# A four-layer graph network on one core: slot waits by tile, layer 3 scaled and added in one VectorE pass, transposes back and stores one tick later

## The chip, the cores and the metric

The kernel runs on one core of a Trainium2 chip. The metric is device time in microseconds (us), the median over several executions. Five engines work from queues of their own, in order: TensorE (PE in the profile, PEld its weight loads), VectorE (DVE), ScalarE (ACT), GpSimd (POOL) and SyncE (SP, which here only issues DMAs). An instruction that waits holds up everything behind it on its engine.

## The reference, cut to what matters

`x` is (16, 1024, 256), `adj` a sparse 1024 x 1024 matrix used by all layers, everything in float32.

```
layer 0: S = sigmoid(relu(x_u W1a + x_v W1b + b1) . W2 + b2)   for every pair u, v
         a = (S * adj)^T x ;  m = (adj^T x) * x
         z = beta1 x + beta2 (a Wa + ba) + beta3 (m Wm + bm)
layer 1: z = z + relu((adj z) W^T + b)
layer 2, 3: f = z W1^T ; s = f . W2 + b2
         c = softmax(leaky_relu(s_i + s_j) + adj) over j
         z = c f + bias2 + z
```

## The kernel before, in words

The first part loads `adj` into `adj_sb`, picks up to 32 edges of every row with VectorE (`slot_a`), and projects four batches on TensorE (`first_group`, `edge_sides`: for each tile of 128 nodes four matmuls, each of which shows as two records, then two ScalarE copies into `st`, and for every second tile three stores `u_d`, `v_d`, `hw_d` on SP's queue). A generator, `work`, deals these tiles out: `more(n)` issues the next n of them. After the row search it has four tiles left. Then come the counts that decide whether the edge lists fit: `full` (L461), two small matmuls (L464, L466), `missed`, a third (L484), and `ok`. Every engine reads `ok` and branches.

The second part (from L683) opens pools of its own on the bytes that the first part's pools gave up. It begins by transposing `adj` (L225, copied into `stage` by L138 and L140), and then works through batches in four groups of four. Beside TensorE's dense work a generator, `Side`, deals out the edge scores of layer 0 at hand-set paces (`PACE`): a gather by GpSimd (L703), two VectorE passes over 128 x 1024 (L820, L822), four ScalarE sums (L826), later a scatter (L708). `paced` ties a step of it to a recent matmul.

A group does layer 0's sums with edges (`with_edges`), layer 1, and then layers 2 and 3 as `front` (projection, L128 with tile `g_wT`) and `sums` (L1089 builds a weight tile `m` on VectorE, L128 with `feats` and `m` sums over eight `jt`). A `sums` covers 512 nodes, so a batch has two, v = 0 and v = 1. At its end `finish` takes four accumulators `acc`, each in a bank of its own of PSUM's eight; column D of an accumulator holds the softmax's denominator.

- Layer 2 (`second`): four reciprocals (L1104), four scaled copies `val` on ScalarE (L1266), and `turn_back`: eight transposes (L1273) and two VectorE adds into `z` (L1277).
- Layer 3 (`third`): the same four reciprocals, scaled copies `st` (L1312), one VectorE add per pair of tiles with the residual that was transposed into PSUM by `early` (L1300, L1316), and a store from ScalarE's queue (L1317).

`later` is a list of steps with countdowns; `tick` counts all of them down and runs those at its head that are due:

```
def tick():
    for what in later:
        what[0] -= 1
    while later and later[0][0] <= 0:
        later.pop(0)[1]()
```

A `front` ticks at jt = 1 and 5, a `sums` at jt = 0, 2, 4 and 6. Besides `turn_back` the list holds `to_row` (due at the next tick) and `from_row` (due at the fifth), which turn a projection's scores into a row.

Of the kernel before, what the change touches and what calls it, by code (L numbers as in the profile page):

```python
# [1 line left out]

# [7 lines left out]
F32 = mybir.dt.float32  # L10
I32 = mybir.dt.int32
U32 = mybir.dt.uint32
AF = mybir.ActivationFunctionType
ALU = mybir.AluOpType
AX = mybir.AxisListType
P = 128
# [15 lines left out]
LEAD = 4  # L32
# [35 lines left out]
def gnn_stack_kernel(  # L68
# [41 lines left out]
    def bank():  # L110
        return psum[-1].tile([P, HN], F32, tag="bank", name="bank")
# [260 lines left out]
    with ExitStack() as stack:  # L372
# [61 lines left out]
        def more(n):  # L434
            for _ in range(n):
                next(work, None)
# [23 lines left out]
        for q in range(NG):  # L460
            nc.vector.tensor_scalar(full[:, q, :], slot_a[:, :, FIRST + QUAD * q], 0.0, None, ALU.is_gt)  # L461
        flags = full.rearrange("p g t -> p (g t)")
        ps = bank()
        nc.tensor.matmul(ps[:, :NF], below, flags, start=True, stop=True)  # L464
        ps2 = bank()
# [14 lines left out]
        nc.vector.tensor_tensor(missed, counts[:, 0:1], counts[:, 1:2], ALU.not_equal)  # L480
        nc.vector.tensor_tensor(missed, missed, counts[:, 3:4], ALU.add)
        nc.vector.scalar_tensor_tensor(missed, counts[:, 2:3], TOP, missed, ALU.is_gt, ALU.add)
        ps3 = bank()
        nc.tensor.matmul(ps3[:, :1], ones, missed, start=True, stop=True)  # L484
        total = prep1.tile([P, NF], F32, name="total")
# [197 lines left out]
    with tc.If(listed > 0) as arm:  # L683
        with ExitStack() as stack:
# [3 lines left out]

            zs = stack.enter_context(tc.tile_pool(name="zs", bufs=2))
            slot_pool = stack.enter_context(tc.tile_pool(name="slots", bufs=LEAD + 2))
            wide_z = stack.enter_context(tc.tile_pool(name="wide_z", bufs=4))
            wide_t = stack.enter_context(tc.tile_pool(name="wide_t", bufs=5))
            psum_pool(stack, "banks", 8)
            gd_pool = stack.enter_context(tc.tile_pool(name="gd", bufs=4))
            gc_pool = stack.enter_context(tc.tile_pool(name="gc", bufs=2))
            put = [Scatters(tc, f"scores {g}") for g in range(NGR)]
            finished = []
            TW = NT * (D + 1)  # L700
# [221 lines left out]
            doing = ["free"]  # L922

            with ExitStack() as first:
                own1 = first.enter_context(tc.tile_pool(name="own1", bufs=1))
                st_pool = first.enter_context(tc.tile_pool(name="st", bufs=2))
                side = Side(score_steps(own1))
                pools = (wide_t, wide_z)
                next_up = load_kept(pools, 0)
                wm = load_wm(own1, nc.sync)  # L930
                zero = own1.tile([P, ZERO], F32, name="zero")
                nc.gpsimd.memset(zero, 0.0)

                def stage(n):
                    return st_pool.tile([P, 2 * 3 * D], F32, tag="st", name="stage")[:, :n]

                def score_free():
                    yield from turn_adj(
                        lambda n: wide_z.tile([P, DH * N], F32, tag="wide", name="stage")
                    )  # L940
                    h, hT = next_up
                    for b in range(B):
                        if b == 1:
                            nat = load_naturals(stage)
                            w1 = load_w1(own1, nc.sync)
                        if b == 2:
                            paced(with_beta2(w1))
                        if b >= GB:
                            yield from edge_sides(st_pool, b, w1, hT)
                        if b == B - 1:  # L950
                            first_hw.extend(load_hw(i) for i in range(GB - 1))
                            first_gd.extend(load_gd(0, 0, ut) for ut in range(4))
                        mT = yield from messages(pools, h, hT)
                        now = hT

                        if b + 1 < GB:
                            h, hT = load_kept(pools, b + 1)
                        elif b + 1 < B:
                            h = load_h(pools[0], b + 1)
                            hT = turned(pools[0], h)  # L960
                            yield 2.4
                        yield from without_edges(pools, b, now, mT, wm)
                        if b == 1:
                            prepare(nat)
                            yield 3

                def with_zeros(main):
                    for n, us in enumerate(main):
                        if 7 < n < 40 or n > 40 and n % 3 == 0:
                            clear()  # L970
                        yield us

                side.along(with_zeros(score_free()))
                assert not zeros

            two = stack.enter_context(tc.tile_pool(name="two", bufs=2))
            three = stack.enter_context(tc.tile_pool(name="three", bufs=3))
            four = stack.enter_context(tc.tile_pool(name="four", bufs=4))


            ea = adj_sb
# [6 lines left out]
            def tick():  # L988
                for what in later:
                    what[0] -= 1  # L990
                while later and later[0][0] <= 0:
                    later.pop(0)[1]()

            def catch_up():
                while later:
                    later.pop(0)[1]()
# [82 lines left out]
            def sums(made, v, finish, early=None):  # L1079

                doing[0] = "sums"
                while "f" not in made:
                    tick()
                f, r, ta = made["f"], made["r"], made["ta"]
                cols = slice(v * HN, (v + 1) * HN)
                acc = [bank() for _ in range(HT)]
                for jt in range(NT):
                    m = four.tile([P, HN], F32, tag="m", name="m")
                    nc.vector.scalar_tensor_tensor(  # L1089
                        m, r[:, cols], ta[:, jt : jt + 1], ea[:, jt, cols], ALU.max, ALU.mult  # L1090
                    )
                    for c in range(HT):
                        product(
                            acc[c][:, : D + 1], m[:, c * P : (c + 1) * P], f[:, jt, :],
                            start=jt == 0, stop=jt == NT - 1,
                        )
                    if jt % 2 == 0:
                        tick()
                    if early:
                        early(v, jt)  # L1100
                    yield 1.7
                share = small.tile([P, HT], F32, tag="share", name="share")
                for c in range(HT):
                    nc.vector.reciprocal(share[:, c : c + 1], acc[c][:, D : D + 1])  # L1104
                finish(v, acc, share)
                yield 1.2

            def exponential(jt):
# [147 lines left out]


            def second(z, i):
                def finish(v, acc, share):
                    cols = slice(v * HN, (v + 1) * HN)  # L1260
                    vals = []
                    for c in range(HT):
                        if c % 2 == 0:
                            pair = four.tile([P, 2, D], F32, tag="st", name="val")
                        val = pair[:, c % 2, :]
                        nc.scalar.activation(val, acc[c][:, :D], AF.Identity, scale=share[:, c : c + 1])  # L1266
                        vals.append(val)

                    def turn_back():
# [6 lines left out]
                        for dh in range(DH):  # L1276
# [1 line left out]
                                z[i][:, dh, cols], ps[dh], gat2.bias2[:, dh : dh + 1], z[i][:, dh, cols],  # L1278
                                ALU.add, ALU.add,
                            )  # L1280
                    later.append([1, turn_back])
                return finish


            def third(z, i, b):
# [17 lines left out]
                            )  # L1303
                    turned_back.append(ps)

                def finish(v, acc, share):
                    for c in range(0, HT, 2):
                        ps = turned_back.pop(0)
                        it = v * HT + c
                        st = four.tile([P, 2, D], F32, tag="st", name="st")  # L1310
                        for k in range(2):
                            nc.scalar.activation(  # L1312
                                st[:, k, :], acc[c + k][:, :D], AF.Identity, scale=share[:, c + k : c + k + 1]
                            )
                        both = st.rearrange("p t d -> p (t d)")
                        nc.vector.tensor_tensor(both, both, ps, ALU.add)  # L1316
                        nc.scalar.dma_start(  # L1317
                            out[b + i, it * P : (it + 2) * P].rearrange("(t p) d -> p t d", p=P), st
                        )
                return finish, early  # L1320

            def pair_layers(b, z, first):
# [13 lines left out]
                yield from sums(m0, 1, *t0)  # L1336
                yield from sums(m1, 0, *t1)
                yield from sums(m1, 1, *t1)
                assert not later

            def group_layers(g, z):

# [25 lines left out]
                        soon(g + 1)  # L1368
                    yield from sums(made[layer, i], 1, *ends)
                loaded.append((hw, nz))  # L1370
                assert not later

            def soon(g):

# [165 lines left out]
```

## Time and profile before

| | us |
|---|---|
| median of 3 runs | 3192.23 (3180.22 to 3192.65) |
| the profiled execution: time, span | 3160.66, 3159.0 |
| TensorE matmul busy | 3089.6 (98%) |
| VectorE busy | 2355.8 (75%) |
| ScalarE busy | 1954.7 (62%) |
| GpSimd busy | 1853.1 (59%) |

The profiled execution was 20 to 32 us shorter than the three timed ones. Busy shares are averages over stages: the first part ends near 110 us, the four groups begin near 953, 1517, 2074 and 2636 us, and the edge scores run beside all but the last.

### The profile page before, as it was taken

How to read it: one execution, taken by the hardware profiler on the slowest of the kernel's cores; microseconds unless marked ns; L12 is line 12 of the kernel's file. 1: busy time of each engine (PE TensorE's matmuls, PEld its weight loads, DVE VectorE, ACT ScalarE, POOL GpSimd, SP SyncE). 2: the span in 40 equal slices, each digit the busy share in tenths (PEclk: the TensorE clock that was granted, in tenths of full speed). 3: DMA queues.
4: the chain of work that ended last, by engine and by line, in shares of the span. 5: the costliest groups of instructions: out<-in, count | busy, mean ns of one | idle time of the engine just before them, and what ended most of it. 6: DMA issues, size and time to landing. Idle time of an engine off the chain costs nothing. (4 is left out here: it accounts for less than half of the span.)

```text
span 3159.0 us, 38968 instructions
## 1 busy us (share of the span) xinstructions
PE 3089.6 (98%) x11954; PEld 2178.2 (69%) x11954; DVE 2355.8 (75%) x3191; ACT 1954.7 (62%) x6512; POOL 1853.1 (59%) x1483
## 2 busy tenths in 40 slices
PE   9899999999999999999999999999999999999999
PEld 5444555545547756888875688888557888858888
DVE  7796777768774678999767899976789982148844
ACT  3245565656667876777987677788667764514242
POOL 1146877667664577767666776756766651076600
PEclk9999999999999999999999999999999999999999
DMA  9799798788889777568877765787765655485500
GB/s 323 286 331 324 251 308 283 256 258 251 259 278 327 229 216 206 150 186 261 294 233 203 207 167 166 262 277 232 223 197 149 162 189 174 130 254 166 165 5 28
DMA packets 288420, 699.96 MB, mean 222 GB/s; under 512 B 46141, under 2 KB 141178, under 8 KB 281034
## 3 DMA queue, kind: packets, MB, share of 16 engines
q0 software_dynamic: 128224, 387.80, 42.1%
q1 hardware_dynamic: 132538, 258.46, 23.5%
q10 hardware_dynamic: 27440, 51.13, 4.3%
q8 instruction: 96, 1.57, 0.2%
q14 instruction: 122, 1.00, 0.1%
HBM read 565.83 MB, written 131.41 MB: 221 GB/s over the span
## 5 line engine op out<-in xcount | busy, mean ns | idle before, releaser
L826 ACT ACTIVATE z<-z 128x256 f32<-128x256 f32 x2432 | 978.9, 405 | 573.3 <-DVE z L822 544.9
L820 DVE TENSOR_TENSOR z<-z,u 128x1024 f32<-128x1024 f32 x608 | 739.0, 1220 | 392.9 <-PE bank L128 284.6
L128 PE MATMUL bank<-feats,m 128*128 128x257 f32 x4096 | 915.5, 381 | 12.8 <-DVE m L1089 7.1
L703 POOL DMA_INDIRECT z<-v_d,slot_v x512 | 652.1, 1274 | 434.8 <-ACT z L826 249.7
L128 PEld LDWEIGHTS bank<-feats,m 128*128 128x128 f32 x4096 | 767.9, 190 | 128.7 <-DVE m L1089 13.4
L708 POOL DMA_INDIRECT dense_d<-gt,slot_at x512 | 665.8, 1300 | 192.7 <-issue 128.9
L822 DVE SCALAR_TENSOR_TENSOR z<-z,w2r 128x1024 f32<-128x1024 f32 x608 | 737.9, 1220 | 9.0
L128 PE MATMUL bank<-gc,hw 128*128 128x256 f32 x2048 | 451.7, 382 | 9.5 <-ACT gc L1120 8.2
L826 ACT ACTIVATION_READ_ACCUMULATOR z<-z 128x1 f32 x2432 | 460.0, 189 | 0.0
L128 PE MATMUL bank<-adj_sb,h 128*128 128x512 f32 x1024 | 444.0, 594 | 2.6 <-ACT st L330 2.6
L128 PEld LDWEIGHTS bank<-gc,hw 128*128 128x128 f32 x2048 | 386.6, 190 | 73.9 <-ACT gc L1120 19.7
L1089 DVE SCALAR_TENSOR_TENSOR m<-rho,tau,adj_sb 128x512 f32<-128x512 f32 x512 | 376.1, 744 | 68.1 <-PE bank L128 65.3
L128 PE MATMUL bank<-adjT_in,y 128*128 128x512 f32 (+1 forms) x960 | 403.3, 580 | 4.6 <-DMA adjT_in<-adjT_d 4.6
L128 PEld LDWEIGHTS bank<-adj_sb,h 128*128 128x128 f32 x1024 | 194.9, 191 | 243.0 <-issue 238.7
L128 PE MATMUL bank<-w,hT 128*128 128x512 f32 (+1 forms) x1024 | 336.8, 490 | 0.0
L128 PEld LDWEIGHTS bank<-adjT_in,y 128*128 128x128 f32 x960 | 182.2, 191 | 219.3 <-issue 200.6
L1120 ACT ACTIVATE gc<-gd 128x1024 f32<-128x1024 f32 x128 | 264.8, 2070 | 88.7 <-PE bank L128 72.7
L128 PEld LDWEIGHTS bank<-w,hT 128*128 128x128 f32 x1024 | 196.1, 192 | 142.5 <-issue 118.8
L128 PE MATMUL bank<-g_wT,z 128*128 128x257 f32 x1024 | 233.7, 380 | 3.4 <-ACT st L1312 2.3
L128 PEld LDWEIGHTS bank<-g_wT,z 128*128 128x128 f32 x1024 | 191.0, 190 | 34.9 <-ACT st L1312 4.3
L703 POOL DMA_INDIRECT z<-v_d,x_node x96 | 119.9, 1249 | 131.6 <-ACT z L826 89.8
L330 ACT ACTIVATE st<-bank 128x512 f32<-128x512 f32 x128 | 75.7, 591 | 103.0 <-PE bank L128 63.4
(168 smaller groups left out, 2369.5 us busy)
## 6 DMA issues: line engine op xcount, KB each, us to landing
gd<-dense_d SPq DMA_DIRECT2D x128, 512.0 KB
dense_d<-zero ACTq DMA_DIRECT2D x64, 512.0 KB
adjT_in<-adjT_d SPq DMA_DIRECT2D x112, 256.0 KB
h<-in_x_dram SPq DMA_DIRECT2D x19, 1024.0 KB
u_d<-st SPq DMA_DIRECT2D x64, 256.0 KB
v_d<-st SPq DMA_DIRECT2D x64, 256.0 KB
hw_d<-st SPq DMA_DIRECT2D x64, 256.0 KB
u<-u_d POOLq DMA_DIRECT2D x32, 512.0 KB
```

The source lines that it names most:

```text
L128: recent.append(nc.tensor.matmul(*args, **kw))
L330: nc.scalar.activation(st[:, c, :2, :], ps.rearrange("p (s k) -> p s k", s=2), AF.Copy)
L703: return nc.gpsimd.indirect_dma_start(out=dst, out_offset=None, in_=src[:], in_offset=bass.IndirectOffsetOnAxis(ap=at, axis=0), **how,)
L708: return nc.gpsimd.indirect_dma_start(out=dst[:], out_offset=bass.IndirectOffsetOnAxis(ap=at, axis=0), in_=src, in_offset=None,)
L820: paced(nc.vector.tensor_tensor(z, z, u, ALU.add))
L822: nc.vector.scalar_tensor_tensor(zk, zk, 0.0, w2r[:, None, :].to_broadcast([P, GB, D]), ALU.max, ALU.mult)
L826: nc.scalar.activation(zk[:, c, :], zk[:, c, :], AF.Copy, accum_out=s[:, k, c : c + 1])
L1089: nc.vector.scalar_tensor_tensor(m, r[:, cols], ta[:, jt : jt + 1], ea[:, jt, cols], ALU.max, ALU.mult)
L1120: paced(nc.scalar.activation(gc, gd.rearrange("p n i -> p i n"), AF.Copy), 16)
```

## The change

Every SBUF pool of the second part (`zs`, `slots`, `wide_z`, `wide_t`, `gd`, `gc`, `own1`, `st`, `two`, `three`, `four`) is opened with `reuse_waits="tile"`. Without it, a pool that lands on bytes of released pools waits, with all its tiles, for every user of those pools. With it, a tile waits for the users of earlier tiles on its own bytes alone. The pool in PSUM stays as it was.

In the first part two tiles of `work` are issued before the first count matmul and one before the third; one is left for the end.

`tick` runs whatever is due, wherever it stands in the list. `turn_back` gets 2 for its countdown instead of 1; layer 2's `finish` makes its four reciprocals itself, as `sums` did, and its `val` tiles grow by the unused column. Layer 3 copies each accumulator with its denominator (257 columns) unscaled on ScalarE, takes the reciprocals of a pair from that copy, and scales and adds the residual in one VectorE pass per tile. Its store goes into `later` with a countdown of 1. What is left in the list at a group's end is run there.

```diff
+        more(2)
         ps = bank()
         nc.tensor.matmul(ps[:, :NF], below, flags, start=True, stop=True)
...
+        more(1)
         ps3 = bank()
         nc.tensor.matmul(ps3[:, :1], ones, missed, start=True, stop=True)
...
-            zs = stack.enter_context(tc.tile_pool(name="zs", bufs=2))
+            zs = stack.enter_context(tc.tile_pool(name="zs", bufs=2, reuse_waits="tile"))
...
-                while later and later[0][0] <= 0:
-                    later.pop(0)[1]()
+                for what in [w for w in later if w[0] <= 0]:
+                    later.remove(what)
+                    what[1]()
...
-                share = small.tile([P, HT], F32, tag="share", name="share")
-                for c in range(HT):
-                    nc.vector.reciprocal(share[:, c : c + 1], acc[c][:, D : D + 1])
-                finish(v, acc, share)
+                finish(v, acc)
...
-                    later.append([1, turn_back])
+                    later.append([2, turn_back])
...
-                        st = four.tile([P, 2, D], F32, tag="st", name="st")
+                        st = four.tile([P, 2, D + 1], F32, tag="st", name="st")
+                        share = small.tile([P, 2], F32, tag="share", name="share")
                         for k in range(2):
-                            nc.scalar.activation(
-                                st[:, k, :], acc[c + k][:, :D], AF.Identity, scale=share[:, c + k : c + k + 1]
-                            )
-                        both = st.rearrange("p t d -> p (t d)")
-                        nc.vector.tensor_tensor(both, both, ps, ALU.add)
-                        nc.scalar.dma_start(
-                            out[b + i, it * P : (it + 2) * P].rearrange("(t p) d -> p t d", p=P), st
-                        )
+                            nc.scalar.activation(st[:, k, :], acc[c + k][:, : D + 1], AF.Copy)
+                        nc.vector.reciprocal(share, st[:, :, D])
+                        for k in range(2):
+                            nc.vector.scalar_tensor_tensor(
+                                st[:, k, :D], st[:, k, :D], share[:, k : k + 1], ps[:, k * D : (k + 1) * D],
+                                ALU.mult, ALU.add,
+                            )
+                        to = out[b + i, it * P : (it + 2) * P].rearrange("(t p) d -> p t d", p=P)
+                        later.append([1, functools.partial(nc.scalar.dma_start, to, st[:, :, :D])])
...
-                assert not later
+                catch_up()
```

More of the change, by code (lines that the diff above doesn't have):

```diff
@@ L1 @@
+import functools
 from contextlib import ExitStack
@@ L684, in gnn_stack_kernel @@
         with ExitStack() as stack:
-            zs = stack.enter_context(tc.tile_pool(name="zs", bufs=2))
-            slot_pool = stack.enter_context(tc.tile_pool(name="slots", bufs=LEAD + 2))
-            wide_z = stack.enter_context(tc.tile_pool(name="wide_z", bufs=4))
-            wide_t = stack.enter_context(tc.tile_pool(name="wide_t", bufs=5))
+            zs = stack.enter_context(tc.tile_pool(name="zs", bufs=2, reuse_waits="tile"))
+            slot_pool = stack.enter_context(tc.tile_pool(name="slots", bufs=LEAD + 2, reuse_waits="tile"))
+            wide_z = stack.enter_context(tc.tile_pool(name="wide_z", bufs=4, reuse_waits="tile"))
+            wide_t = stack.enter_context(tc.tile_pool(name="wide_t", bufs=5, reuse_waits="tile"))
             psum_pool(stack, "banks", 8)
-            gd_pool = stack.enter_context(tc.tile_pool(name="gd", bufs=4))
-            gc_pool = stack.enter_context(tc.tile_pool(name="gc", bufs=2))
+            gd_pool = stack.enter_context(tc.tile_pool(name="gd", bufs=4, reuse_waits="tile"))
+            gc_pool = stack.enter_context(tc.tile_pool(name="gc", bufs=2, reuse_waits="tile"))
             put = [Scatters(tc, f"scores {g}") for g in range(NGR)]
@@ L924, in gnn_stack_kernel @@
             with ExitStack() as first:
-                own1 = first.enter_context(tc.tile_pool(name="own1", bufs=1))
-                st_pool = first.enter_context(tc.tile_pool(name="st", bufs=2))
+                own1 = first.enter_context(tc.tile_pool(name="own1", bufs=1, reuse_waits="tile"))
+                st_pool = first.enter_context(tc.tile_pool(name="st", bufs=2, reuse_waits="tile"))
                 side = Side(score_steps(own1))
@@ L974, in gnn_stack_kernel @@
                 assert not zeros
-            two = stack.enter_context(tc.tile_pool(name="two", bufs=2))
-            three = stack.enter_context(tc.tile_pool(name="three", bufs=3))
-            four = stack.enter_context(tc.tile_pool(name="four", bufs=4))
+            two = stack.enter_context(tc.tile_pool(name="two", bufs=2, reuse_waits="tile"))
+            three = stack.enter_context(tc.tile_pool(name="three", bufs=3, reuse_waits="tile"))
+            four = stack.enter_context(tc.tile_pool(name="four", bufs=4, reuse_waits="tile"))
             ea = adj_sb
@@ L1258, in second, with finish @@
             def second(z, i):
-                def finish(v, acc, share):
+                def finish(v, acc):
                     cols = slice(v * HN, (v + 1) * HN)
+                    share = small.tile([P, HT], F32, tag="share", name="share")
+                    for c in range(HT):
+                        nc.vector.reciprocal(share[:, c : c + 1], acc[c][:, D : D + 1])
                     vals = []
@@ L1263, in finish @@
                         if c % 2 == 0:
-                            pair = four.tile([P, 2, D], F32, tag="st", name="val")
-                        val = pair[:, c % 2, :]
+                            pair = four.tile([P, 2, D + 1], F32, tag="st", name="val")
+                        val = pair[:, c % 2, :D]
                         nc.scalar.activation(val, acc[c][:, :D], AF.Identity, scale=share[:, c : c + 1])
@@ L1304, in early, with finish @@
                     turned_back.append(ps)
-                def finish(v, acc, share):
+                def finish(v, acc):
                     for c in range(0, HT, 2):
@@ L1370, in group_layers @@
                 loaded.append((hw, nz))
-                assert not later
+                catch_up()
             def soon(g):
```

## The prediction

> **What bounds the kernel now.** I read the busy shares first, then TensorE's waits, then the timeline around the largest of them.
>
> ```profile
> span 3159.0 us, 38968 instructions
> PE 3089.6 (98%) x11954; PEld 2178.2 (69%) x11954; DVE 2355.8 (75%) x3191; ACT 1954.7 (62%) x6512; POOL 1853.1 (59%) x1483
> ```
>
> TensorE is busy for 98%, so the change can only give what TensorE idles or runs slowly: 3159.0 - 3089.6 = 69 us, of which some 7.5 are the first loads and 7 the tail. Who holds it, from the waits of engine PE (total, times, longest):
>
> ```profile
> PE bank L128 <- ACT st L1312: 8.4, 13, 1.5
> PE bank L1273 <- ACT val L1266: 7.4, 6, 2.2
> PE bank L128 <- DVE m L1089: 7.1, 8, 2.3
> PE bank L464 <- DVE full L461: 4.0, 1, 4.0
> PE bank L225 <- ACT stage L140: 2.8, 1, 2.8
> PE bank L484 <- DVE total L486: 1.5, 1, 1.5
> ```
>
> Rows 1 and 2 are the layers' ends, rows 4 to 6 the passage from the first part to the second. The timeline of that passage (start, duration, idle before and releaser):
>
> ```profile
> 94.41 0.38 PE L464 MATMUL bank<-full,below 128*128 128x32 f32 x2 [4.04 <-DVE full L461]
> 96.49 0.56 PE L484 MATMUL bank<-missed,ones 128*128 128x1 f32 x2 [1.48 <-DVE total L486]
> 96.91 13.30 PE L128 MATMUL bank<-w,hT 128*128 128x512 f32 x32
> 117.15 3.06 PE L225 MATMUL bank<-ident,adj_sb 128*128 128x128 f32 x26 [2.75 <-ACT stage L140]
> ...
> 115.57 0.69 DVE L138 COPY stage<-bank 128x512 f32<-128x512 f32 x1 [13.34 <-DMA hw_d<-st]
> ```
>
> TensorE waits 4.04 us for counts while four independent tiles lie behind them. Those then take 13.30 us for 32 records; earlier, 64 records took 20.80, so 10.4 would do: 2.9 us run at a slower clock. VectorE then waits 13.34 us to copy into `stage` until the last store of a tile it has no business with has landed. The windows show the same (length, TensorE busy, clock, DMA share):
>
> ```profile
> 90.00:100.00 10.00, 4.48 (x12) 2.46 (x11) 9.07 (x42) 0.52 (x2) 0.94 (x2) 0.78 0.31 112
> 100.00:105.00 5.00, 5.00 (x14) 3.11 (x13) 2.23 (x3) 1.58 (x3) 0.90 (x4) 0.76 0.00 0
> 130.00:140.00 10.00, 10.00 (x24) 4.37 (x23) 10.00 (x18) 0.00 (x0) 0.00 (x0) 1.00 1.03 420
> ```
>
> The last two figures of a row are DMA share and GB/s: DMA idles around 100 us and is full (1.03) from 120 to 180.
>
> **What the Trainium skill says.** "TensorE: Matmul & The Clock Gate", Part 1, states that an idle window of about 3.4 us halves TensorE's clock until a similar busy one has passed. The trace agrees: after the 4.04 us, records started 0.86 us apart instead of 0.43, and the granted clock is 0.78 and 0.76. "DMA: Bandwidth & Descriptors", Issuing engines are not separate DMA queues, says that moving an issue between queues adds no bandwidth; the full DMA row above agrees, so an earlier start helps only by filling the idle stretch. No page bears on pool waits.
>
> **Part 1, the passage.** *Removed:* with two tiles first, TensorE runs from 90.37 for 2 x 2.6 = 5.2 us to 95.6; `full` was ready at 94.26. The two count matmuls take 0.6, the third tile 2.6, L484 0.56, the last tile 2.6: end at 101.9 instead of 110.2, 8.3 earlier (4.04 + 1.48 + 2.9). `ok` comes at about 99.4 instead of 98.35, still before TensorE's end, so the branch costs nothing new; VectorE's last count lines slip 1.2 us under TensorE's tile. The moved tiles take along two ScalarE copies each (0.60 and 0.38 us, ScalarE idles 9.97 there) and SP's three stores per pair (0.36 to 0.46 each, SP idle).
>
> *The pool wait:* `stage` can be copied once its bank is full, at 103.3 instead of 115.57; the gaps of 0.47 and 2.75 go. TensorE would begin the next stage 8.3 + 3.2 = 11.5 us sooner. But GpSimd's gathers still read `v_d` and wait for its last store, issued at about 103.3 instead of 110.42: 7 to 9 us sooner. And VectorE's `wm` (L150) waited at 126.06 for a load behind about 5.5 MB of others (15.7 us at 350 GB/s, worked out from the issues between 110 and 126): it lands some 8 us sooner, no more. From 126 to 156 VectorE ran without a gap, and TensorE waited 3.88 us at 152.8 for its `mT` (L350). So VectorE's 8 us, not TensorE's 11.5, may pass on: that wait grows to about 7. Bounds: 5 (GpSimd and VectorE late, clock lost again) to 17 (the stall at 152.8 goes too: 3.9 idle and 1.9 at the slow clock). I take **-9.5**, between the two chains.
>
> *The later pools* (`two`, `three`, `four`) are first used near 1088 us, long after `own1` and `st` were last used (near 950): 0, hidden by 100 us of `with_edges`.
>
> **Part 2, layer 3.** ScalarE: 128 copies of 257 columns at 384 ns (row L1010) for 128 scaled ones at 465 (L1312): 10 us less in all. VectorE, with times from start to start: 64 reciprocals of two columns (0.13) for 128 of one (0.13): -8; 128 passes of 256 columns from PSUM at 0.43 (L1143: 54.7 us for 128) for 64 adds at 0.66 (L1316: 42.5 for 64): +12. Together +4, at the unoverlapped means (480, 683, 156 ns) +7: at most 0.25 us per `finish`. VectorE's idle time in layer 3 of the first three groups is 135 - 128.8 = 6.2, 140 - 132.2 = 7.8 and 180 - 148.6 = 31 us, for eight ends each: it covers 8 x 0.25 = 2.
>
> The gain is that the copies no longer wait for VectorE, whose reciprocals stand behind L820 or L822. That frees banks, row 1's 8.4 us. But in the trace the copies also stand behind a batch of L826 on ScalarE (at 1952.5 to 1954.1, with L1312 at 1954.12 and a stall of 1.39), and that order may stay. Bounds: -8 (all) to +7 (none, VectorE's extra bare). The new wait: VectorE's reciprocal now waits for ScalarE's two copies, with `m` and L820 behind it, and TensorE behind `m`; L1316 had to wait for those copies too (4.3 us, 9 times), so I count nothing more. I take **-2**.
>
> **Part 3, `turn_back`.** For v = 0 it sat behind `from_row`, due at jt = 2; with 2 it is due at jt = 2 as well: 0. For v = 1 it moves from jt = 1 of the next `front` to jt = 5, its eight transposes and two VectorE adds (741 ns) behind four projections of 0.87 us. But banks go round in order, as `front`'s stalls on L1312 at its third tile show (1969.22, 1.9 us after its start at 1967.3). At the largest stall
>
> ```profile
> 1296.26 0.42 ACT L826 ACTIVATE z<-z 128x256 f32<-128x256 f32 x1 [0.48 <-DVE z L822]
> ...
> 1297.87 1.18 ACT L1266 ACTIVATE val<-bank,share 128x256 f32<-128x256 f32 x3
> ...
> 1298.38 0.44 PE L1273 MATMUL bank<-ident,val 128*128 128x128 f32 x2 [2.16 <-ACT val L1266]
> ```
>
> the third projection takes the transposes' place at 1296.22 and needs the accumulator that the same `val` frees at 1298.33. The stall changes its name: **0** (bounds -6.3, the five stalls of v = 1, to +2 if banks come later still).
>
> **Part 4, stores.** 64 issues of 0.38 us leave ScalarE's queue for one tick later, past L826 and `front`'s copies; ScalarE stood 6.8 us behind L1316 for them, off the path. At the very end they run at once. There the last copy came at 3152.95, delayed by a reciprocal behind L1316 and by the first store; without that, and with two short passes after it: **-0.5** (-1 to +0.5).
>
> **Sum.** -9.5 - 2 + 0 - 0.5 = -12: from the profiled execution's 3160.7 to 3148.7. The runs shown lie 20 to 32 us above that execution for a reason the profile doesn't show; I put the same difference to their median, 3192.2 - 12 = 3180. That is 0.38%, below the 0.5% (16 us) that a measurement of this kernel can tell from no change.
>
> **The rivals.**
> *All stalls go* (0.38): the passage gives 17, rows 1 and 2 give 8 and 6, less 3 for VectorE: -28, 3164. For it: ScalarE's copies lose a real dependency, so they may be placed ahead of L826. Against: VectorE is 95% busy in those windows, and a stall removed there turns into a wait for `m`.
> *VectorE held at every layer-3 end* (0.11), slower: the reciprocal waits behind ScalarE's L826 batch (1297.87 - 1296.26 = 1.6 us) and two copies (0.77), with 0.25 of extra work: 2.6 us per `finish`. In groups 1 and 2 the idle time covers 6.2 + 7.8 = 14 of 16 x 2.6 = 42: +28, less 12: +16, 3208. It decides from 1.6 us per `finish` on (16 x 1.6 - 14 = 12). For it: 95% busy. Against: L1316 has waited for the same copies and lost only 4.3 us in all.
> *The pool option does nothing* (0.05): the first gathers and loads need the same stores, and only the 8.3 us of reordering stay, eaten by `mT`: -4, 3188.
>
> **How the numbers follow.** My forecast, 3180, has 0.46. The range 3158 to 3198 holds it with its bounds, the first rival with 6 us below for the spread of the runs, and a third of the slower one. Faster by over 0.5%: the first rival and a tenth of my forecast, 0.43; slower by over 0.5%: 0.09; between, 0.48.
>
> **What would show it.** Right: no gap above 0.5 us on TensorE from 85 to 110 and the clock at 1.00 there; L225 begins near 102; the first L138 near 103 with no wait for `hw_d`; a longer wait for `mT`, 5 to 8 us, near 145; `front`'s third tile waiting for `val`. Wrong: L138 still waiting for `hw_d`; row 2 gone with nothing in its place; PE's wait for `m` well above 7.1 us; a reciprocal in layer 3 that waits over 20 us in total for ScalarE.

## The result and the profile after

The kernel with the change takes 3161.1 us (median of six executions, 3157.2 to 3169.1), the kernel before beside it 3188.5 (six, 3180.2 to 3192.7): ratio 0.9918, 95% interval 0.9901 to 0.9936. In a later comparison (e5 below), with 18 and 37 executions, the same pair gave 3151.2 and 3160.2: 0.9969 (0.9957 to 0.9981). So the change makes the kernel faster by 0.2 to 1.0%; the two intervals don't meet, and a section below says what is known of that. The forecast, 3180 of 3192.2, is a ratio of 0.9962 and lies between them; 3161.1 is in its range, near the lower end. Faster by over 0.5%, as in the first comparison, had been given 0.43, and a change within 0.5%, as in the second, 0.48.

The profiled execution after took 3164.1 us, 3.4 more than the profiled one before, which had been 28 us below its median. The two profiles therefore can't be subtracted as wholes. They can be read stage by stage. Line numbers of the kernel after are 1 to 5 higher than before: L128 is now L129, L1089 is L1093, L1312 is L1317. The busy shares first:

```profile
span 3162.6 us, 39016 instructions
PE 3092.3 (98%) x11954; PEld 2180.8 (69%) x11954; DVE 2360.7 (75%) x3191; ACT 1945.9 (62%) x6512; POOL 1876.9 (59%) x1483
```

VectorE has 4.9 us more work, ScalarE 8.8 us less: the prediction had +4 to +7 and -10. Then TensorE's waits (total, times, longest):

```profile
PE bank L129 <- DVE m L1093: 10.9, 12, 1.9
PE bank L129 <- DVE mT L351: 10.2, 3, 4.7
...
PE bank L129 <- ACT st L1317: 3.9, 3, 2.2
...
PE bank L1277 <- ACT val L1270: 1.0, 1, 1.0
```

The rows for `full`, `total` and `stage` are gone, and `val` has nearly gone (7.4 to 1.0). `st`, which had been at the top, fell from 8.4 to 3.9. Two rows grew in their place: `m` from 7.1 to 10.9 and `mT` from 4.4 to 10.2. The passage between the parts, from the timelines of TensorE and of VectorE:

```profile
96.75 0.30 PE L466 MATMUL bank<-full,below 128*128 128x32 f32 x2
96.89 0.39 PE L468 MATMUL bank<-full,ones 128*128 128x32 f32 x2
97.11 2.83 PE L129 MATMUL bank<-w,hT 128*128 128x512 f32 x8
99.77 0.28 PE L487 MATMUL bank<-missed,ones 128*128 128x1 f32 x2
99.91 2.83 PE L129 MATMUL bank<-w,hT 128*128 128x512 f32 x8
103.22 7.21 PE L226 MATMUL bank<-ident,adj_sb 128*128 128x128 f32 x64 [0.47 <-ACT st L332]
...
142.23 3.70 PE L129 MATMUL bank<-mT,wm 128*128 128x512 f32 x8 [1.61 <-DVE mT L351]
149.81 5.49 PE L129 MATMUL bank<-mT,wm 128*128 128x512 f32 x6 [3.88 <-DVE mT L351]
155.09 20.32 PE L129 MATMUL bank<-adj_sb,h 128*128 128x512 f32 x46
```

```profile
103.97 0.69 DVE L139 COPY stage<-bank 128x512 f32<-128x512 f32 x1 [0.43 <-issue]
...
119.18 0.49 DVE L151 TENSOR_SCALAR wm<-wm,beta 128x512 f32<-128x512 f32 x1 [8.54 <-DMA wm<-in_L_gnn_Wm_dram]
...
141.50 0.67 DVE L351 TENSOR_TENSOR mT<-bank,hT 128x512 f32<-128x512 f32 x1
...
149.07 0.69 DVE L351 TENSOR_TENSOR mT<-bank,hT 128x512 f32<-128x512 f32 x1
```

No count matmul waits any more; eight records take 2.83 us, and the clock is 1.00 in the windows from 80 to 110 us; the transposes of `adj` run as one stretch of 64. VectorE copies at 103.97 in place of 115.57. But at 110.6 it comes to `wm` and stands 8.54 us for its load; everything behind it, the first `mT` too, is that much later. TensorE now waits twice for `mT`, 1.61 us at 142.23 and 3.88 us at 149.81, where the first profile of the kernel before has one wait:

```profile
156.70 4.54 PE L128 MATMUL bank<-mT,wm 128*128 128x512 f32 x6 [3.88 <-DVE mT L350]
```

The wait of 1.61 us is what the late `wm` leaves: TensorE comes to the third `mT` before VectorE does. The one of 3.88 us is not. In all 14 profiles VectorE starts the fourth `mT` 7.57 us after the third, with other instructions between them, while TensorE's eight records between them take 3.6 to 3.7 us; the wait is 3.88 or 3.89 us in 13 of the 14. The windows there (length, the five engines' busy times, clock, DMA share, GB/s):

```profile
140.00:150.00 10.00, 4.50 (x11) 1.62 (x10) 10.00 (x16) 0.86 (x5) 0.00 (x0) 0.95 1.05 347
150.00:160.00 10.00, 10.00 (x17) 4.24 (x18) 9.80 (x13) 4.26 (x21) 2.91 (x3) 0.70 1.05 410
```

After two waits TensorE is busy 4.5 of 10 us, and in the next 10 the clock is 0.70, as the Trainium skill says of idle windows in "TensorE: Matmul & The Clock Gate", Part 1. The six records behind the second wait, to the start of the second dense batch, take 5.28 us, where they took 4.37 in the kernel before; in e7, after a wait of 3.53 us at this place, the clock stayed at 1.00 and they took 2.68. VectorE is busy for all of the first window: TensorE follows it here.

### The profile page after: what moved, and what is told of

Same layout as the page of the kernel before. It is cut to its first block, busy times and chain, and to the rows that moved or that the text cites. A ratio compares the mean times of both kernels' runs of the same rounds, so it can differ in the third digit from the quotient of the medians.

```text
span 3162.6 us, 39016 instructions
## 1 busy us (share of the span) xinstructions
PE 3092.3 (98%) x11954; PEld 2180.8 (69%) x11954; DVE 2360.7 (75%) x3191; ACT 1945.9 (62%) x6512; POOL 1876.9 (59%) x1483
## 5 line engine op out<-in xcount | busy, mean ns | idle before, releaser
L129 PE MATMUL bank<-feats,m 128*128 128x257 f32 x4096 | 919.5, 382 | 16.1 <-DVE m L1093 10.9
L129 PEld LDWEIGHTS bank<-feats,m 128*128 128x128 f32 x4096 | 768.8, 190 | 134.6 <-DVE m L1093 20.8
L711 POOL DMA_INDIRECT dense_d<-gt,slot_at x512 | 680.8, 1330 | 190.8 <-issue 136.2
L129 PE MATMUL bank<-gc,hw 128*128 128x256 f32 x2048 | 452.4, 382 | 11.0 <-ACT gc L1121 10.1
L129 PE MATMUL bank<-adj_sb,h 128*128 128x512 f32 x1024 | 442.9, 593 | 3.3 <-DMA h<-in_x_dram 1.6
L129 PEld LDWEIGHTS bank<-gc,hw 128*128 128x128 f32 x2048 | 386.9, 191 | 76.1 <-ACT gc L1121 18.7
L1093 DVE SCALAR_TENSOR_TENSOR m<-rho,tau,adj_sb 128x512 f32<-128x512 f32 x512 | 376.7, 747 | 67.1 <-PE bank L129 64.4
L129 PE MATMUL bank<-adjT_in,y 128*128 128x512 f32 (+1 forms) x960 | 403.9, 581 | 6.1 <-DMA adjT_in<-adjT_d 2.8
L129 PEld LDWEIGHTS bank<-adj_sb,h 128*128 128x128 f32 x1024 | 194.5, 190 | 243.8 <-issue 240.5
L129 PE MATMUL bank<-w,hT 128*128 128x512 f32 (+1 forms) x1024 | 335.5, 488 | 0.9 <-ACT z L829 0.9
L129 PEld LDWEIGHTS bank<-adjT_in,y 128*128 128x128 f32 x960 | 182.0, 191 | 221.6 <-issue 204.5
L129 PEld LDWEIGHTS bank<-w,hT 128*128 128x128 f32 x1024 | 194.8, 191 | 142.9 <-issue 120.6
L129 PE MATMUL bank<-g_wT,z 128*128 128x257 f32 x1024 | 232.5, 381 | 2.5 <-issue 2.5
L129 PEld LDWEIGHTS bank<-g_wT,z 128*128 128x128 f32 x1024 | 193.2, 191 | 33.2 <-issue 6.3
L711 POOL DMA_INDIRECT dense_d<-gt,x_at x96 | 121.0, 1261 | 29.3 <-issue 27.1
```

The lines of the kernel that those rows point to most:

```text
L129: recent.append(nc.tensor.matmul(*args, **kw))
L711: return nc.gpsimd.indirect_dma_start(out=dst[:], out_offset=bass.IndirectOffsetOnAxis(ap=at, axis=0), in_=src, in_offset=None,)
L1093: nc.vector.scalar_tensor_tensor(m, r[:, cols], ta[:, jt : jt + 1], ea[:, jt, cols], ALU.max, ALU.mult)
```

## The experiments

The first four ran on one chip with the kernel before (3175.3 us), the next four on a second (3160.2), the last four on a third (3173.9). Ratios are against the kernel before on the same chip. "Layer 2" and "layer 3" lengths below are read off TensorE's records in the profile and added over the first three groups: from a group's first sum with `m` to its first transposition of `z`, and from there to the next group's first matmul with `gc`.

**e1, the kernel before, once more.**

> The kernel before, unchanged, profiled again. Theory P (its profiled execution of 3160.7 us was an unusually short one): this profile shows a span of 3175 to 3195 us, and the ratio is 1.000. Theory Q (an execution under the profiler is 20 to 30 us shorter for this kernel): the span is 3155 to 3165 us again, while its times stay near 3188.

Measured: 3180.9 us, ratio 1.0014 (0.9996 to 1.0032), and a profiled span of 3178.8 us with the same code whose first profile had 3159.0. Where they differ most: layer 1 of the last group (116.2 and 123.9 us) and of the first (152.6 and 157.2), and the groups' edges. None of these is touched by the change. This is theory P: the first profile was a short one. So two profiles may differ by 20 us in stages that have nothing to do with an edit, and only the stages with the edit in them are compared below.

**e2, the passage alone:** all pools by tile, and the two calls of `more`.

```diff
+        more(2)
...
+        more(1)
...
-            zs = stack.enter_context(tc.tile_pool(name="zs", bufs=2))
+            zs = stack.enter_context(tc.tile_pool(name="zs", bufs=2, reuse_waits="tile"))
```

> The kernel before with the passage's half of the change: all pools of the second part wait by tile, and the count matmuls come behind two tiles and one tile of the first part. Layers 2 and 3 as before. Theory A (the passage gives nearly all): 20 to 27 us less, ratio 0.992 to 0.994. Theory B (as the prediction sized it, the passage gives some 10 us and the layers' ends the rest): ratio 0.9965 to 0.998.

Measured: 3170.9 us, 0.9983 (0.9972 to 0.9995), about -5 us. The first part ends at 103.1 us in place of 110.7, the second dense batch begins at 155.0 in place of 161.1. That is far from theory A; the gain is a little smaller than theory B's range (0.9965 to 0.998).

**e3, layers 2 and 3 alone,** pools and order of the first part as before:

```diff
-                    later.append([1, turn_back])
+                    later.append([2, turn_back])
...
+                            nc.scalar.activation(st[:, k, :], acc[c + k][:, : D + 1], AF.Copy)
+                        nc.vector.reciprocal(share, st[:, :, D])
```

> The kernel before with the other half alone: layer 3's unscaled copies and one VectorE pass, its stores one tick later, transposes back at the second tick, and tick running all that is due. Theory A: ratio 0.998 to 1.001. Theory B: 14 to 18 us less, ratio 0.9945 to 0.9955, and TensorE's waits for L1312 and L1266, 15.8 us together before, fall under 6.

Measured: 3170.1 us, 0.9978 (0.9966 to 0.9989), about -7 us. TensorE's waits fell as theory B had it, to 4.4 us for `st` and 0.9 for `val`, but the time fell by half of its 14 to 18 us, just outside theory A's range. Layer 2 is 488.2 us (before: 498.9), layer 3 is 386.3 (before: 373.1).

**e4, layer 3 alone:** as e3, with `turn_back` left at 1.

```diff
-                    later.append([2, turn_back])
+                    later.append([1, turn_back])
```

> As the layers' half, but the transposes back keep their countdown of 1: layer 3's copies, its VectorE pass and later stores, and the new tick. If layer 3 gives the gain of the layers' half: the same ratio as that half within 0.001. If the later transposes give it: ratio 0.998 to 1.001. The prediction had -2 us for this and 0 for the transposes.

Measured: 3177.7 us, 1.0000 (0.9988 to 1.0012). By time layer 3's part gives nothing; what e3 gave is `turn_back`, which I had put at nothing. In this profile layer 3 takes 384.8 us, 11.7 more than in the kernel before. The time doesn't show such a loss; why is open.

**e5, the full change beside more executions.**

> The full change beside its halves' sum on the same footing. Theory A (parts add up: passage about -5, layers about -7): ratio 0.9955 to 0.9970. Theory B (the parts need each other, as the first comparison of the full change, 0.9918, suggests): 0.9905 to 0.9935.

Measured: 3151.2 us, 0.9969 (0.9957 to 0.9981). Theory A: -0.0017 and -0.0022 of the halves add up to 0.9961, within the interval; theory B is outside it.

**e6, the later transposes alone:** `turn_back` at 2 and the `tick` that it needs, nothing else.

> The kernel before with turn_back's countdown at 2 alone (and the new tick, which it needs); layer 3 and pools as before. Theory A (the transposes alone carry what layers 2 and 3 gave together, because four banks are free there for front's projections): ratio 0.9970 to 0.9985, TensorE's wait for val from 7.4 us to under 2, layer 2 of the first three groups 6 to 9 us shorter in all, layer 3 stages within 1 us of before. Theory C (the stall changes its name, as the prediction had it): 0.9993 to 1.0005, with a new wait at front's third projection. If layer 3's single pass gives something by itself, this run must be slower than the two together (0.9978) by 0.001 or more; if it costs, faster.

Measured: 3152.8 us, 0.9970 (0.9954 to 0.9986), -7.4 us by the medians and -9.5 by the ratio. TensorE's wait for `val` is 1.6 us, layer 2 is 491.1 us. Layer 3 is 376.0, 2.9 over the kernel before where 1 was allowed, though the edit doesn't touch it. With turn_back at 1 (before, e1, e2, e4, e9) layer 2 is 495.0 to 501.2 us, with 2 (nine profiles) 488.1 to 491.1: the two sets don't meet. Theory C, the prediction's own, falls. Against e3, on another chip, the ratio is lower by 0.0008 with overlapping intervals, so the comparison of this run with both parts together settles nothing.

**e7, the full change without layer 3's part:** e2 and e6 together.

> The full change without layer 3's part: passage and later transposes, layer 3 scaled, added and stored as before. Theory D (layer 3's pass costs, since a reciprocal now waits for ScalarE with m behind it): 0.001 to 0.003 below the full change, its layer 3 stages 124, 126 and 123 us in place of 127, 126 and 127, TensorE's wait for m near 5 in place of 10.9 us and for st near 8. Theory E (layer 3's pass gives 2 us, as predicted): 0.0005 to 0.001 above the full change.

Measured: 3148.2 us, 0.9959 (0.9944 to 0.9974), 0.0010 below e5 with intervals that overlap: by time, theories D and E are not told apart. The profile says D, in its waits (shown below) and in its layer 3 of 374.9 us against 380.3.

**e8, the full change with `wm` scaled later:** the load stays, the scaling comes after the first batch's messages.

```diff
-                wm = load_wm(own1, nc.sync)
+                wm = own1.tile([P, DH, D], F32, name="wm")
+                nc.sync.dma_start(wm, g0_Wm.rearrange("(c p) k -> p c k", p=P))
...
+                        if b == 0:
+                            nc.vector.tensor_scalar(wm, wm, beta3, None, ALU.mult)
```

> The full change with VectorE's scaling of wm (L151) emitted after the first batch's messages, where wm is first needed, and its load where it was. Theory W (the 8.54 us that VectorE stands at 110.6 for wm are what returns half of the passage's gain through mT): TensorE's wait for mT from 10.2 to under 6 us, the second dense batch 4 to 6 us earlier, 0.001 to 0.002 below the full change. Theory X (DMA is full there, the next load takes over): the wait for mT turns into one for h or hT of the same size, within 0.0005 of the full change.

Measured: 3146.7 us, 0.9944 (0.9923 to 0.9966), 4.6 us below e5 by the medians, with overlapping intervals. VectorE's wait in the passage, from its waits between 103 and 160 us:

```profile
DVE mT L351 <- DMA adjT_d<-stage: 7.0, 1, 7.0
```

The wait for `wm` is gone, and 7.0 of its 8.5 us come back under another name: the first `mT` needs a buffer that `stage` held, whose store lands at 124.6. TensorE's first wait for `mT` is gone (2.2 us in e5); the 3.9 us at 147.4 stay, as in nearly every run. The wait for `mT` is 6.3 in all (theory W: under 6), and the second dense batch begins 3.3 us sooner than in e5 (W: 4 to 6). So W and X are each half right: with DMA full at a share of 1.03 from 110 us on, the wait for one transfer gave way to that for another. How much the edit gives is not shown by one profile: in e7, with `wm` scaled where it was, VectorE waited only 5.9 us for it and the second batch began at 149.25, before the 151.81 of e8. The Trainium skill's "DMA: Bandwidth & Descriptors", Issuing engines are not separate DMA queues, says that moving issues between engines adds no bandwidth; no run here moves one, so that is not tested.

**e9, the pool option alone:** all `reuse_waits="tile"`, no `more`.

> The kernel before with the pools' option alone, the four tiles still dealt out at the end. Theory F (the option removes VectorE's 13.34 us wait and TensorE's 2.75 us, and the moved tiles the other 8 us of the first part): L225 begins within 0.5 us of 110.2, one L138 copy about 1 us later with no wait for hw_d, the second dense batch begins 1 to 4 us sooner than in the kernel before (161.1), ratio 0.9988 to 1.0. Theory G (the option carries the whole passage): the second batch 6 us sooner, ratio near 0.9983, as with both. Rival that the option does nothing: VectorE still waits 13 us at L138.

Measured: 3176.2 us, 1.0009 (0.9996 to 1.0021). VectorE's waits between 105 and 160 us:

```profile
DVE stage L138 <- PE bank L225: 9.0, 1, 9.0
DVE wm L150 <- DMA wm<-in_L_gnn_Wm_dram: 8.2, 1, 8.2
```

The wait for `hw_d` is gone, so the option does what it says. But with the tiles dealt out at the end there is nothing to copy until TensorE gets to L225 at 110.2 us, and the wait for `wm` grows from 3.8 to 8.2. The second dense batch begins at 160.7, 0.4 us sooner than before: theory F's description with less than its gain of 1 to 4 us, and a ratio that allows no gain above 0.0004.

**e10, layer 3's VectorE work one tick later.**

```diff
+                        def scale_and_add(st=st, ps=ps, to=to):
+                            share = small.tile([P, 2], F32, tag="share", name="share")
+                            nc.vector.reciprocal(share, st[:, :, D])
...
+                        later.append([1, scale_and_add])
```

> The full change with layer 3's reciprocals and scale-and-add passes put into the list with a countdown of 1 as well; ScalarE's copies stay at the end of the sums, the store follows one tick after the pass. Theory H (place: VectorE's work at the sums' end stands ahead of the next m): TensorE's wait for m from 12 us to under 7, the layer 3 stages of the first three groups from 380 us to 372 to 376 in all, 0.001 to 0.002 below the full change. Theory I (amount: VectorE has no room for 16 x 0.3 us more anywhere): 379 to 383 us, the wait for m still over 10, within 0.0007 of the full change. Slower still if the two banks held one tick longer matter: a new wait of front on L1317 or of the transposes for a bank.

Measured: 3156.2 us, 0.9946 (0.9927 to 0.9964); wait for `m` 12.7 us, layer 3 377.9 us. At the ends compared, those of the first and third group, VectorE's records stand in the same order as in e5, so the edit didn't move what it was meant to move, and it tells nothing between H and I. It serves as one more profile of the full change, and its ratio as a third measure of it.

**e11, reciprocals from the accumulators again,** the scale-and-add pass kept:

```diff
+                    for c in range(HT):
+                        nc.vector.reciprocal(share[:, c : c + 1], acc[c][:, D : D + 1])
...
-                        nc.vector.reciprocal(share, st[:, :, D])
```

> The full change with layer 3's reciprocals taken from the accumulators (four of one column, as before the change) and the scale-and-add pass kept. Theory J (the cost is the reciprocal that waits for ScalarE's copies, 19.3 us in all): the reciprocals' wait for st gone, the passes wait for st instead by less than half of it, layer 3 stages from 380 to 374 to 377 us. Theory I (amount): 380 to 384 us, since 8 x 2 more instructions of 0.13 us come on VectorE, and the wait for m stays over 10 us.

Measured: 3151.3 us, 0.9937 (0.9914 to 0.9959). VectorE's wait for the copies and TensorE's for `m`, first in e5, then in e11:

```profile
DVE share L1318 <- ACT st L1317: 19.3, 11, 6.2
PE bank L129 <- DVE m L1093: 12.7, 16, 1.9
```

```profile
DVE st L1321 <- ACT st L1319: 1.9, 7, 0.4
PE bank L129 <- DVE m L1093: 7.1, 11, 1.6
```

VectorE now has 64 instructions more than in the full change (3255 in place of 3191), and yet layer 3 takes 376.1 us, and TensorE waits 5.6 us less for `m`. That is against theory I: the amount of VectorE's work is not what costs. The numbers are those of theory J, but its reason doesn't hold as it was put: of the 19.3 us that reciprocals waited for copies in e5, none lie inside layer 3 of the first two groups, where most of the waits for `m` inside layer 3 are (6.1 of 7.7 us). There it is the order on VectorE that changes, as told below. By time e11 and e10, the full change's order on the same chip, are 0.0009 apart with overlapping intervals.

**e12, e7 and e8 together:** passage, later transposes, late `wm`, layer 3 as before.

> Passage, later transposes and the later scaling of wm, with layer 3 as before: the two edits that looked best put together. If they add up: 0.001 to 0.003 below the full change, about 0.9935 to 0.9950 of before; layer 3 stages 374 to 376 us. If neither was more than the spread of the runs: equal to the full change, 0.9960 to 0.9975.

Measured: 3153.6 us, 0.9938 (0.9915 to 0.9961), inside the first of the two expectations and outside the second. That doesn't show that the edits add up: e10, which amounts to the full change, is inside the first as well. The full change itself didn't run on this chip, so e10, e11 and e12 (0.9946, 0.9937, 0.9938) can be compared with one another, and their intervals overlap. Against the full change on one chip only e7 and e8 stand, 3.1 and 4.6 us lower, within the intervals. None of them is shown to beat it.

## Why the prediction was right, and where it was not

**The passage: right in its mechanism, the sum too high by some 4 us.** The order of the tiles did what was worked out: TensorE at full clock through the counts, transposes at 103.2 (102 was expected), copies at 103.97 without the wait for `hw_d`, the first part 7.5 us shorter (of 8.3 worked out). The waits for `mT` grew to 5.5 us between 103 and 200 us from 3.9, but not as foreseen: the old wait stayed at 3.88 and one of 1.61 came before it. TensorE began the sums 8.6 us sooner (112.05 for 120.70) and not 11.5, as the load of `h` held it 1.63 us, which wasn't in the working. The term at fault is the -9.5 taken between TensorE's chain and VectorE's: VectorE's alone decides. `wm` landed at 119.2 in place of 126.1, 6.9 us sooner and not 8; TensorE's records at 149.81 are 6.9 sooner than those at 156.70 in the kernel before; 0.9 went into the slower clock behind them, and 6 are left at the second batch. By time the passage is 5.4 us (e2), at the lower of my two bounds. On average that lasts: the first group's `gc` matmuls start at 951.3 to 957.1 us in the six profiles with the old order of the tiles (mean 954.1), at 940.7 to 954.7 in the eight with the new (948.8); the two sets overlap. The rival that the pool option does nothing is half right: by itself it gives nothing (e9), where in place of the 13.34 us that looked largest VectorE waits 9.0 us for TensorE's transposes and 4.4 more for `wm`. The order of the tiles without the option wasn't tried, so how the 6 us divide between them when both are there stays open.

**The transposes: wrong, 0 predicted, about -7 to -9.5 measured.** The step that failed is what was drawn from "banks go round in order": that the third projection, in the transposes' place, needs an accumulator that `val` frees. TensorE's timeline after, at the end where the kernel before had its largest stall:

```profile
1288.76 8.19 PE L129 MATMUL bank<-feats,m 128*128 128x257 f32 x37
1296.78 5.38 PE L129 MATMUL bank<-g_wT,z 128*128 128x257 f32 x24
1301.99 1.03 PE L1277 MATMUL bank<-ident,val 128*128 128x128 f32 x8
1302.87 1.90 PE L129 MATMUL bank<-g_wT,z 128*128 128x257 f32 x8
```

Six projections (24 records) run in one stretch after the sums' end at 1296.78. The third of them starts about 1.7 us later, while ScalarE's `val` copies begin only at 1300.1. So it didn't need the accumulators that `val` frees. The trace doesn't number the banks; by the program four are held there, and in layer 2 the other four of the eight serve `front`. I had inferred the order from stalls of `front` at its third tile in layer 3, but there `early` holds two of those four. When the transposes come at 1301.99, `val` is there. Row 2's 7.4 us go with nothing in their place but 1.0 us, one of the prediction's own signs of being wrong.

**Layer 3: a small gain predicted, none measured, a cost in the profiles.** -2 was predicted, with bounds of -8 and +7; by time e4 says 0.0 with an interval of 3.8 us on each side. By its length layer 3 is slower: 372.5 to 377.8 us in the seven profiles with the old layer 3, 377.9 to 386.4 in the six with the new one. The gain that I priced came: TensorE's wait for `st` is 6.5 to 10.4 us in the seven profiles with the old layer 3 and 3.6 to 5.4 in the six with the new one, 4 to 5 us less. At 1966.64 `front` ran all its 32 records without a stop, where the kernel before stopped at 1969.90:

```profile
1966.64 7.11 PE L129 MATMUL bank<-g_wT,z 128*128 128x257 f32 x32
```

The cost that I did not price came too, with a second sign of being wrong: over the whole kernel the wait for `m` is 3.5 to 7.1 us in the seven and 9.6 to 14.1 in the six. TensorE's waits within layer 3 alone, the first three groups added (us), separate it best:

| kernel | for `st` | for `m` |
|---|---|---|
| before | 7.6 | 0.0 |
| e7, old layer 3 | 8.9 | 0.2 |
| the full change | 3.9 | 8.4 |
| e5, the full change again | 4.1 | 7.7 |
| e11, reciprocals from the accumulators | 4.2 | 3.0 |

ScalarE's gain of 4 us is there and TensorE pays 8 for it. The sentence at fault is that L1316 had waited for the copies too, "so I count nothing more". In the timeline of e5 at one end in the first group:

```profile
1472.84 1.18 ACT L1317 ACTIVATE st<-bank 128x257 f32<-128x257 f32 x4
1472.91 0.74 DVE L1093 SCALAR_TENSOR_TENSOR m<-rho,tau,adj_sb 128x512 f32<-128x512 f32 x1
...
1473.57 1.21 DVE L825 SCALAR_TENSOR_TENSOR z<-z,w2r 128x1024 f32<-128x1024 f32 x1
1474.71 0.22 DVE L1318 RECIPROCAL share<-st 128x2 f32<-128x2 f32 x2
...
1475.03 1.64 DVE L1320 SCALAR_TENSOR_TENSOR st<-st,share,bank 128x256 f32<-128x256 f32 x4
1476.59 1.21 DVE L823 TENSOR_TENSOR z<-z,u 128x1024 f32<-128x1024 f32 x1
...
1477.86 1.21 DVE L825 SCALAR_TENSOR_TENSOR z<-z,w2r 128x1024 f32<-128x1024 f32 x1
...
1479.06 1.40 DVE L1093 SCALAR_TENSOR_TENSOR m<-rho,tau,adj_sb 128x512 f32<-128x512 f32 x2
...
1479.85 0.48 PE L129 MATMUL bank<-feats,m 128*128 128x257 f32 x1 [1.88 <-DVE m L1093]
```

VectorE has no idle time in these 6 us. The reciprocals, all four passes (1.64 us, where two adds took 1.28) and three passes of the edge scores stand in its queue ahead of the next `m`, and TensorE has waited 1.88 us when that comes. From the start of the last `m` before the passes of such an end to that of the next `m`, VectorE takes on average (seven ends a group) 5.2, 5.0 and 3.9 us in groups 0, 1 and 2 before, and 6.4, 5.5 and 4.4 after: 0.5 to 1.2 us per end, where I had 0.25. In e11 it is 5.0, 5.4 and 5.0, so only group 0 is back at its old length, and the waits for `m` within layer 3 fall to 3.0 us. Why group 2 lost none in spite of its 5.0 stays open. The idle time of 6.2 to 31 us that I let cover the extra work lies elsewhere, not at the ends.

So VectorE does hold TensorE at the ends, as in my slower rival, but by its queue and not by waiting for ScalarE, and for 8 us in place of 42. The sign that I had set for it, reciprocals waiting over 20 us, was nearly met (19.1 us, ten times) by waits that say little: 9.3 us of them lie in the last group, where no edge scores run, and 6.2 are one wait at the end of the group before.

**The stores: the step came, the gain didn't.** -0.5 was predicted. The last store is issued 1.41 us after the last matmul's end in the six profiles with the new layer 3, 1.81 or 1.82 in the seven with the old one. But from that matmul's end to the span's end it is 6.2 to 6.7 us in the seven and 6.3 to 7.7 in the six (6.6 before, 7.4 after, 7.7 in e5).

**The sum.** -9.5 - 2 + 0 - 0.5 = -12 was forecast. The parts measured -5.4 (e2), 0.0 (e4) and about -7 (e3 less e4) or -9.5 (e6): -12 to -15. The sum held because two errors cancelled: too much in the passage, nothing in the transposes. The full change measured -9 on one chip (e5), what amounts to it -17 on another (e10), and -27 came out of the first comparison. That 27 is close to the first rival's 28, but its mechanism isn't there, as `m` and `mT` wait more than before. What differs is above all the kernel before: 3188.5 us there, 3160 to 3175 on the three other occasions, while the full change moved only from 3161 to 3151. Why it was slow there was not settled; e1 shows where such 20 us can lie.

## What to carry to other kernels

Before a stall is written off as one that only changes its name, count the banks that are held at that very place; an order inferred from another stage, where more are held, can mislead. When a copy is freed of a reciprocal, look at where the reciprocal and what hangs on it now stand in the other engine's queue, and what is behind them: here ScalarE's 4 us came back as 8 of `m`. A large wait that is removed at a passage can be worth only what the next transfer in a full DMA queue gains: here 13.34 us went and 6 came out. And a wait that is nearly as long in every run, such as the 3.88 us for `mT`, need not come from a stall further up; look for what stands between the two instructions on the engine that is waited for.

## What was not expected of the hardware

The same code differs by more between occasions (3160 to 3188 us in medians of the kernel before) than the change is worth, so ratios on one chip are the only measure of it. One source is visible in the trace: in the full change's first profile, at 718 us, VectorE waited 4.7 us for a gather of GpSimd with `mT` behind it, and TensorE waited 4.7 us for that; in e7 TensorE had no wait in that stretch.
